# Four-layer cross-attention stack: second half of layer 0 and first FFN fed by runs and block transposes

## The chip, the cores and the metric

The kernel runs on one core of one Trainium2 chip, as one launch. The metric is device time in microseconds (us), the median of several runs. TensorE (PE) does matrix products and 128x128 transposes through the identity, VectorE (DVE), ScalarE (ACT) and GpSimd (POOL) do the rest, and SyncE (SP) issues most DMA transfers, in order.

## The reference, cut to what matters

Eight batches of 128 tokens by 512 features, f32, pass through four layers. Each layer adds a cross attention over a context of the same shape and then an FFN, each fed by a layernorm of the running x.

```python
for layer in range(4):
    x = x + xattn[layer](layernorm(x), ctx)
    x = x + ffn[layer](layernorm(x))

# layer 0's attention: h = layernorm(x)
r = h * rsqrt(mean(h * h) + 1e-5) * ln_weight
q, k, v = r @ w_q.T, ctx @ w_k.T, ctx @ w_v.T        # 32 heads of 128
s = q @ k.T + position_bias                          # per head
p = where(mask, softmax(where(mask, s, -inf)), 0)
out = h + (p @ v).reshape(B, S, 4096) @ w_out.T

# layer 0's FFN: y = layernorm(x)
out = y @ W_base.T + b_base + sum over 8 experts of
      sparsemax(y @ W_router.T)[e] * (y @ lora_A[e]) @ lora_B[e]
```

Layer 1 is a channel attention with small projections and an int8 linear FFN, layer 2 a grouped-query attention with rotary positions (32 heads over 8) and an FFN whose NF4 weights (512 by 1376) are quantised and dequantised in the kernel, layer 3 an attention with normed queries and keys and a gated FFN of low-rank experts.

## The kernel before

The residual lies in on-chip memory as eight tiles `x[b]` of 128 tokens by 512. Products contract over partitions, so every input of a projection is needed with features on the partitions: `ctxT` holds the context of all batches that way ([128, 4 chunks, 8 x 128 tokens]), and the tiles `xT`, made for half the batches at a time, the normed x.

The main loop runs over units. A unit is one head of layer 0's attention (`Unit0`) or layer 2's (`Unit2`) for one half of four batches; the list goes by kind, half, group of four heads, head, so units 0 to 31 are layer 0 with batches 0 to 3 and units 32 to 63 layer 0 with batches 4 to 7. The loop is pipelined: at unit u it projects keys and queries of unit u+3, scores unit u+2, sends that unit's probabilities to DRAM as 32x32 blocks and reads those of u+1 back transposed (`far`, then `pt`), and multiplies unit u's with the values. The first three units take no such detour: their probabilities are transposed by PE (L226) right behind the softmax (L404 to L408). After each fourth head come four projections of values and four output projections.

All that isn't such a unit runs as side work. A table maps slot numbers to functions (`put(i, f)`), and `slot()`, called after each projection and around the values and output projections, runs what stands at the present number and then some NF4 items at a pace (`NF4_PACE`) that differs between stages and between a full and an empty table. `l0_half(1)` fills the table at u = 3 with the preparation of the second half of layer 0; `short_stages(0)` fills it after unit 31 with the first FFN (`F0`), the whole of layer 1 (`L1`, `F1`) and the inputs of layer 2 (`L2Inputs`) for batches 0 to 3, `short_stages(1)` after unit 63 for the other half. `drain()` runs what is left, at u = 29, 61 and 93. The framework orders instructions within each engine anew and places semaphores, so an engine's order is not the program's order word for word, but each engine runs its own list strictly in order.

What the change touches, with the line numbers of the kernel before:

- `transposed` (L187 to L192) makes four PE transposes into one bank, L191.
- `load_ctx` and `l0_ctx` (L354): one load of a batch's context, four PE transposes, an ACT copy into `ctxT` (L355).
- `l0_query` (L366): load of x, `layernorm` (L173: statistics and scaling on DVE, the inverse root on POOL at L160), the rms norm `l0_rms` (L361 a square on ACT, L362 and L364 on DVE), and on POOL x += h (L371).
- `l0_turn` (L374): four PE transposes of the normed rows, and L375 on DVE, which multiplies them by `ln_weight` into `xT0[1]`.
- `norm_sent` and `norm_arrives` (from L258): layernorm, block transpose on DVE (L262), to DRAM, and back in four transfers to a block tile `xB`, features on partitions. It serves later stages already.
- `norm_pieces` (L1193): layernorm in one slot, four PE transposes and an ACT copy (L1200) in the next.
- `l0_half` (L1214), `short_stages` (L1227), and the two first tiles `xT0`, with three warm-up matmuls on the second (L1297 to L1302).

Of the kernel before, what the change touches and what calls it, by code (L numbers as in the profile page):

```python
# [11 lines left out]
F32 = mybir.dt.float32  # L12
# [11 lines left out]
P = 128  # L24
B = 8
D = 512
DC = D // P
NG = 8
HALF = 4
# [33 lines left out]
def kernel(ctx: ExitStack, tc: tile.TileContext, a, out):  # L63
    nc = tc.nc
    V, S, G, T = nc.vector, nc.scalar, nc.gpsimd, nc.tensor

    def pool(name, bufs, **kw):
        return ctx.enter_context(tc.tile_pool(name=name, bufs=bufs, **kw))
# [10 lines left out]
    dram = pool("scratch", 1, space=DRAM)  # L79
# [32 lines left out]
    def load(dst, src):  # L112
        nc.sync.dma_start(dst, src)
# [19 lines left out]
    def along(v, n):  # L133

        return v.unsqueeze(2).to_broadcast([v.shape[0], v.shape[1], n])
# [5 lines left out]
    def batches(hf):  # L141
        return range(hf * HALF, (hf + 1) * HALF)

    def cols(b):
        return slice((b % HALF) * P, (b % HALF + 1) * P)

    def toks(b):
        return slice(b * P, (b + 1) * P)
# [9 lines left out]
    def inv_sqrt(v, shape):  # L158

        return G.tensor_tensor(v, v, mhalf.to_broadcast(shape), ALU.pow)  # L160
# [3 lines left out]
    for b in range(B):  # L164
        t = keep.tile([P, D], F32, name=f"x{b}")
        x.append(t)

    ctxT = keep.tile([P, DC, B * P], F32, name="ctxT")
    lnw = keep.tile([P, DC], F32, name="lnw")
# [5 lines left out]
    def layernorm(st, b):  # L175
        stats = st.small(6, "st")
        V.bn_stats(stats, x[b])
        mv = st.small(2, "mv")
        V.bn_aggr(mv, stats)
        rs = st.small(1, "rs")  # L180
        V.tensor_scalar(rs, mv[:, 1:2], 1e-5, None, ALU.add)  # L181
        inv_sqrt(rs, [P, 1])
        h = st.wide("h")
        V.tensor_scalar(h, x[b], mv[:, 0:1], rs, ALU.subtract, ALU.mult)
        return h

    def transposed(st, src):  # L187

        tp = st.tp()
        for c in range(DC):  # L190
            T.transpose(tp[:, c, :], src[:, c * P:(c + 1) * P], ident)  # L191
        return tp  # L192

    def xt_tile():
        return xtp.tile([P, DC, 512], F32, tag="xT", name="xT")
# [8 lines left out]
    def load_ctx(st, b):  # L204
        c = st.wide("h")
        load(c, a["ctx_4096"][b])
        return c
# [48 lines left out]


    def norm_sent(st, b, quarters=False):  # L258
        h = layernorm(st, b)
        view = "p (a b k) -> p a b k" if quarters else "p (b a k) -> p a b k"  # L260
        tb = st.wide("sq" if st.name == "s" else "pt", (P, 4, DC, 32))
        V.transpose(tb, h.rearrange(view, a=4, k=32))  # L262
        far = dram.tile([4, 32, 4, P], F32, tag="farn", name="far", bufs=4)
        load(far.rearrange("a i b n -> (a i) (b n)"), tb.rearrange("p b c j -> p (b c j)"))
        return far

    def norm_arrives(xB, b, far):
        i = 4 * (b % HALF)
        for q in range(4):
            load(xB[32 * q:32 * q + 32, i:i + 4].rearrange("p a c j -> p a (c j)"), far[:, :, q, :].rearrange("a i n -> i a n"))  # L270

    def xb_tile():
        return xtp.tile([P, 16, DC, 32], F32, tag="xT", name="xB")
# [19 lines left out]
    class Unit:  # L293
# [26 lines left out]
        def send(self):  # L320
            self.arrive = blocks_sent(qkv, self.p, "0", (1, 2))
# [30 lines left out]
            V.tensor_reduce(anyv, m8, AX.X, ALU.max)  # L352

    def l0_ctx(st, b):  # L354
        S.copy(ctxT[:, :, toks(b)], transposed(st, load_ctx(st, b)))  # L355

    def l0_rms(st, h):

        r = st.wide("sq")
        ss = st.small(1, "ss")  # L360
        S.activation(r, h, AF.Square, accum_out=ss)  # L361
        V.tensor_scalar(ss, ss, 1.0 / D, 1e-5, ALU.mult, ALU.add)  # L362
        done = inv_sqrt(ss, [P, 1])
        V.tensor_scalar(r, h, ss, None, ALU.mult)  # L364
        return r, done

    def l0_query(st, b):
        load(x[b], a["x"][b])
        h = layernorm(st, b)
        r, _ = l0_rms(st, h)  # L370
        G.tensor_add(x[b], x[b], h)  # L371
        return r

    def l0_turn(st, b, r):  # L374
        V.tensor_mul(xT0[b // HALF][:, :, cols(b)], transposed(st, r), along(lnw, P))  # L375
# [769 lines left out]
    with ExitStack() as early:  # L1145
# [13 lines left out]
        side = Stream("s", sub_pool("side", 2), ps, {k: ("side", 3) for k in ("mm", "tp", "sc", "pv", "po")})  # L1159
# [5 lines left out]
        xT0, xT2 = [], []  # L1165
# [6 lines left out]
        def put(i, f, *args):  # L1172
            table.setdefault(i, []).append((f, args))
# [20 lines left out]
        def norm_pieces(i, box, b, get, lag=1):  # L1194

            def norm():
                box[b] = layernorm(side, b)

            def turn():
                S.copy(get()[:, :, cols(b)], transposed(side, box[b]))  # L1200

            put(i, norm)
            put(i + lag, turn)

        def norm_blocks(i, b, get, quarters=False):

            box = {}

            def send():
                box[b] = norm_sent(side, b, quarters)  # L1210

            put(i, send)
            put(i + 2, lambda: norm_arrives(get(), b, box[b]))

        def l0_half(hf):
            box = {}

            def query(b):
                box[b] = l0_query(side, b)

            now[0] = 0
            for i, b in enumerate(batches(hf)):
                put(4 * i, l0_ctx, side, b)
                put(4 * i + 1, query, b)
                put(4 * i + 3, lambda b: l0_turn(side, b, box[b]), b)

        def short_stages(hf):  # L1227
            o = {}
            now[0] = 0

            def begin(name, kind, *args):
                o[name] = kind(side, *args)

            def call(i, name, method, *args):
                put(i, lambda: getattr(o[name], method)(*args))

            put(0, begin, "f0", F0, hf)
            box = {}
            for i, b in enumerate(batches(hf)):
                norm_pieces(i, box, b, lambda: o["f0"].xT)  # L1240
                call(i + 3, "f0", "route", b)
                call(i + 9, "f0", "hidden", b)
                call(i + 11, "f0", "output", b)
            call(7, "f0", "gate")
            put(14, lambda: o["f0"].pool.__exit__(None, None, None))
            put(15, begin, "l1", L1, hf)

            for i, b in enumerate(batches(hf)):
                t = 16 + 15 * i
                call(t - 1, "l1", "norm", b)  # L1250
                call(t, "l1", "project", b)
                call(t + 8, "l1", "project_values", b)
                for n, s in enumerate((2, 6, 10, 13)):
                    call(t + s, "l1", "score", b, n)
                    call(t + s + 4, "l1", "arrive", b, n)
                    call(t + s + 9, "l1", "weigh", b, n)
                call(t + 23, "l1", "close", b)
                call(t + (29 if i < 3 else 24), "l1", "output", b)
            t = 16 + 15 * 3 + 24
            put(t, lambda: o["l1"].pools.close())  # L1260
            put(t + 1, begin, "f1", F1, hf)
            def last():
                o["xT"] = (xb_tile, xt_tile)[hf]()
                xT2.append(o["xT"])

            box2 = {}
            put(t + 6, last)
            for i, b in enumerate(batches(hf)):
                call(t + 1 + i, "f1", "norm", b)
                call(t + 3 + i, "f1", "turn", b)  # L1270
                call(t + 4 + i, "f1", "output", b)

                if hf == 0:
                    norm_blocks(t + 6 + i, b, lambda: o["xT"])
                else:
                    norm_pieces(t + 6 + i, box2, b, lambda: o["xT"], 2)
            t = t + 7
            put(t, lambda: o["f1"].pool.__exit__(None, None, None))
            if hf == 0:
                put(t + 1, begin, "l2", L2Inputs)  # L1280
                for b in range(B):
                    call(t + 1 + b, "l2", "gather", b)
                    call(t + 5 + b, "l2", "turn", b)
                put(t + 13, lambda: o["l2"].pool.__exit__(None, None, None))
# [9 lines left out]

        for unit in units[:3]:
            unit.far = False
        xT0 += [xt_tile(), xt_tile()]  # L1297

        V.memset(xT0[1][:, 0, :], 0.0)
        idle = side.mm()  # L1300
        for i in range(3):
            T.matmul(idle, lhsT=xT0[1][:, 0, 0:P], rhs=xT0[1][:, 0, :], start=True, stop=True)  # L1302
        of = {b: (main, side)[b // 2] for b in batches(0)}
        cts = {b: load_ctx(of[b], b) for b in batches(0)}
        for b in batches(0):
# [24 lines left out]
        for u, unit in enumerate(units):  # L1330
            stage[0] = u // (4 * NG)
            turning[0] = 8 * NG - 4 <= u < 8 * NG
            if u == 3:
                l0_half(1)
# [98 lines left out]
    n = len(items)  # L1433
# [117 lines left out]
```

## Time and profile before

| what | us |
|---|---|
| median of 3 runs | 3042.48 (3041.72 to 3043.21) |
| the profiled run's own time | 3044.83 |
| its span | 3042.7 |
| DVE busy | 1901.7 |
| ACT busy | 1347.2 |
| POOL busy | 382.7 |
| granted TensorE clock, mean | 0.999 |

The span is the time from the first to the last recorded instruction of the core; the run's own time also holds what lies around it. Durations in the views below come from that one profiled execution. Lines with an x and a number are groups; a name such as `ctxT<-tp` is output and input. Text in brackets behind an instruction says how long its engine had been idle and what ended the wait.

### The profile page before, as it was taken

Reading aid. Unit: us, or ns where it says so; the run is one execution under the profiler, and the core shown is the slowest. Engines: PE = TensorE matmul, PEld = TensorE weight load, DVE = VectorE, ACT = ScalarE, POOL = GpSimd, SP = SyncE. Lnnn points to the kernel's source line nnn. Section 1 sums busy time; section 2 is a strip of 40 time slices with the busy share of each in tenths; the row PEclk is TensorE's granted clock in tenths of the full one; section 3 lists DMA queues with packets and bytes.
Section 4 is the critical chain, followed back from the end, with each engine's and each line's share of the span. In section 5 each row is a group of like instructions: output and inputs, shape, how many; then the busy total and the mean of one; then the engine's idle time right before and its main releaser. Section 6 shows DMA issues by size and latency. Waiting matters only on the chain.

```text
span 3042.7 us, 35209 instructions
## 1 busy us (share of the span) xinstructions
PE 3011.0 (99%) x10668; PEld 1648.4 (54%) x10672; DVE 1901.7 (63%) x3830; ACT 1347.2 (44%) x3793; POOL 382.7 (13%) x491
## 2 busy tenths in 40 slices
PE   9999999999999999999999999999999999999999
PEld 4544555544444565555555554446666565565554
DVE  5766677667776566887888882215555455555554
ACT  4555565546552533555555660003333434333332
POOL 2000000101110122332111110001111111111110
PEclk9999999999999999999999999999999999999999
DMA  7434444336555633655344443224555655655540
GB/s 217 136 115 125 124 130 125 101 118 166 169 167 165 188 104 103 180 178 178 109 150 132 120 124 95 75 74 144 160 188 176 187 166 169 192 166 178 171 125 14
DMA packets 452796, 433.90 MB, mean 143 GB/s; under 512 B 47968, under 2 KB 343648, under 8 KB 452096
## 3 DMA queue, kind: packets, MB, share of 16 engines
q1 hardware_dynamic: 418432, 355.08, 38.6%
q10 hardware_dynamic: 23040, 41.95, 4.6%
q0 software_dynamic: 11136, 34.61, 3.8%
q8 instruction: 87, 1.43, 0.2%
q14 instruction: 101, 0.83, 0.1%
HBM read 311.93 MB, written 119.56 MB: 142 GB/s over the span
## 4 chain that ended last, share of the span: by engine, by line
PE 86%; DVE 8%; ACT 2%; issue 1%; DMA 1%; POOL 0%; SPq 0%; DVEq 0%; ACTq 0%; POOLq 0%
PE mm L282 18%; PE mm L219 12%; PE po L219 7%; PE mm L417 7%; PE tp L988 7%; PE mm L1011 7%; PE mm L946 5%; PE pv L1071 4%; PE sc L1048 4%; PE pv L330 3%; PE sc L310 3%; PE mm L955 2%; PE mm L714 1%; ACT s L214 1%; PE mm L724 1%
## 5 line engine op out<-in xcount | busy, mean ns | idle before, releaser
L219 PE MATMUL mm<-w,o 128*128 128x512 f32 x1024 | 464.3, 597 | 2.0 <-ACT o L332 1.6
L780 ACT ACTIVATE ind<-nw,bounds 128x512 f32<-128x512 f32 (+2 forms) x495 | 345.1, 712 | 239.1 <-DVE dq L791 162.7
L282 PE MATMUL mm<-xT,w 128*128 128x512 f32 x768 | 346.8, 594 | 3.5 <-DVE rot L704 2.2
L791 DVE SCALAR_TENSOR_TENSOR dq<-ind,dq 128x512 f32<-128x512 f32 (+2 forms) x462 | 327.4, 709 | 27.1 <-ACT ind L780 9.1
L219 PEld LDWEIGHTS mm<-w,o 128*128 128x128 f32 x1024 | 189.2, 191 | 222.4 <-issue 208.0
L214 ACT ACTIVATE s<-s,nm 128x128 f32<-128x128 f32 x512 | 198.2, 388 | 99.0 <-DVE nm L301 94.5
L282 PEld LDWEIGHTS mm<-xT,w 128*128 128x128 f32 x768 | 142.5, 190 | 170.2 <-issue 162.3
L1011 PE MATMUL mm<-w,xT 128*128 128x512 f32 x512 | 233.9, 592 | 0.0
L219 PE MATMUL po<-w,o 128*128 128x512 f32 x512 | 233.2, 594 | 0.0
L282 PE MATMUL mm<-ctxT,w 128*128 128x512 f32 x512 | 230.6, 593 | 1.3 <-ACT ctxT L1306 0.7
L417 PE MATMUL mm<-w,ctxT 128*128 128x512 f32 x512 | 230.5, 593 | 0.0
L214 ACT ACTIVATE p<-sc,nm,rq 128x256 f32<-128x256 f32 x256 | 141.2, 563 | 115.9 <-DVE nm L1053 111.9
L310 PEld LDWEIGHTS sc<-k,q 128*128 128x128 f32 x1024 | 131.5, 191 | 53.0 <-issue 45.1
L219 PEld LDWEIGHTS po<-w,o 128*128 128x128 f32 x512 | 96.3, 190 | 110.6 <-issue 103.1
L417 PEld LDWEIGHTS mm<-w,ctxT 128*128 128x128 f32 x512 | 95.2, 190 | 112.0 <-issue 110.3
L160 POOL TENSOR_TENSOR rs<-rs,mhalf 128x1 f32<-128x1 f32 x64 | 37.8, 593 | 934.1 <-DVE rs L181 923.6
L946 PE MATMUL mm<-xB,w 128*128 128x512 f32 (+1 forms) x352 | 152.3, 592 | 0.8 <-DVE x L220 0.8
L220 DVE TENSOR_TENSOR x<-x,mm 128x512 f32<-128x512 f32 x128 | 86.6, 677 | 104.7 <-PE mm L219 104.5
L1052 DVE TENSOR_REDUCE nm<-sc 128x2 f32<-128x512 f32 x128 | 85.3, 674 | 101.7 <-PE sc L1048 101.4
L282 PEld LDWEIGHTS mm<-ctxT,w 128*128 128x128 f32 x512 | 93.4, 190 | 101.2 <-issue 97.9
L1011 PEld LDWEIGHTS mm<-w,xT 128*128 128x128 f32 x512 | 97.0, 190 | 89.5 <-issue 85.4
L332 ACT COPY o<-pv 128x512 f32<-128x512 f32 x128 | 74.2, 580 | 158.5 <-PE pv L330 158.4
(261 smaller groups left out, 4883.8 us busy)
## 6 DMA issues: line engine op xcount, KB each, us to landing
w<-in_l_wq SPq DMA_DIRECT2D x128, 256.0 KB
w<-in_l_wo SPq DMA_DIRECT2D x128, 256.0 KB
far<-tb SPq DMA_DIRECT2D x125, 256.0 KB
pt<-far SPq DMA_DIRECT2D x500, 64.0 KB
far<-tb SPq DMA_DIRECT2D x60, 512.0 KB
pt<-far SPq DMA_DIRECT2D x240, 128.0 KB
far<-tb SPq DMA_DIRECT2D x63, 384.0 KB
pt<-far SPq DMA_DIRECT2D x252, 96.0 KB
```

The lines of the kernel that those rows point to most:

```text
L214: S.activation(dst(h), src(h), AF.Exp, bias=negm[:, h:h + 1], scale=by, accum_out=su[:, h:h + 1])
L219: T.matmul(mm, lhsT=o(h), rhs=wo[h], start=h == 0, stop=h == 3)
L282: T.matmul(mm, lhsT=w[:, c, :], rhs=chunk(xT, c), start=c == 0, stop=c == DC - 1)
L310: T.matmul(sc[:, i, :], lhsT=self.q[:, i * P:(i + 1) * P], rhs=k[:, i * P:(i + 1) * P], start=True, stop=True)
L417: T.matmul(mm, lhsT=ctxT[:, c, toks(self.hf * HALF + i)], rhs=grp.wv[c], start=c == 0, stop=c == DC - 1)
L780: S.activation(ind, w, AF.Relu, bias=bounds[:n, i:i + 1], scale=(down + up)[i][1])
L791: V.scalar_tensor_tensor(dst, ind, step, dst, ALU.min, ALU.subtract if i == len(down) else ALU.add)
L946: T.matmul(mm[:n, :], lhsT=w[c][:, j * P:j * P + n], rhs=chunk(xT, c), start=c == 0, stop=c == DC - 1)
L988: T.matmul(it.kv[:, s, :], lhsT=lhsT, rhs=it.wkv[c // 2][:, c % 2, :], start=c == 0, stop=c == DC - 1)
L1011: T.matmul(mq, lhsT=self.xT[it.hf][:, c, cols(it.b)], rhs=it.wq[c], start=c == 0, stop=c == DC - 1)
L1048: T.matmul(sc[:, i, :], lhsT=it.qT[2 * j + i], rhs=it.kT, start=True, stop=True)
L1071: T.matmul(pv, lhsT=it.v[:, j, :], rhs=it.pts[j], start=j == 0, stop=j == 1)
```

## The change

Three things are done differently for parts of the work.

The context of batches 4 to 7 is read straight from the input in runs of 128 bytes, by four transfers a batch (`runs_back`), so that each 32x32 block lies where one block transpose on DVE (`runs_turned`) leaves it transposed in `ctxT`.

The rms-normed rows of these batches are block-transposed on DVE (`blocks_out`, split out of `norm_sent`), sent to DRAM, read back in four transfers into a block tile (`norm_arrives`), and multiplied there by `ln_weight` on POOL (`l0_weigh`). `xT0[1]` becomes such a block tile. The steps of one batch are now spread over ten slots and batches start six slots apart; before, it was four slots each.

In the first FFN of batches 0 to 3 (`hf == 0`) the layernormed rows go to DRAM whole (`runs_sent`), come back two slots later in runs of 128 bytes, and are block-transposed two slots after that (`norm_runs`). All later slots of `short_stages(0)` move by three; `short_stages(1)` stays as it was. In the loop over `L1` a variable is renamed because `s` is now the shift.

```diff
--- before.py
+++ after.py
@@ -256,8 +256,9 @@
 
 
     def norm_sent(st, b, quarters=False):
-        h = layernorm(st, b)
-        view = "p (a b k) -> p a b k" if quarters else "p (b a k) -> p a b k"
+        return blocks_out(st, layernorm(st, b), "p (a b k) -> p a b k" if quarters else "p (b a k) -> p a b k")
+    def blocks_out(st, h, view):
         tb = st.wide("sq" if st.name == "s" else "pt", (P, 4, DC, 32))
         V.transpose(tb, h.rearrange(view, a=4, k=32))
         far = dram.tile([4, 32, 4, P], F32, tag="farn", name="far", bufs=4)
@@ -268,6 +269,25 @@
         i = 4 * (b % HALF)
         for q in range(4):
             load(xB[32 * q:32 * q + 32, i:i + 4].rearrange("p a c j -> p a (c j)"), far[:, :, q, :].rearrange("a i n -> i a n"))
+    def runs_sent(src, queue):
+        far = dram.tile([P, D], F32, tag="farr", name="far", bufs=4)
+        queue.dma_start(far, src)
+        return far
+    def runs_back(st, far, queue):
+        t = st.wide("h", (P, DC, 4, 32))
+        src = far.rearrange("(k j) (c a e) -> a j c k e", j=32, c=DC, e=32)
+        for q in range(4):
+            queue.dma_start(t[32 * q:32 * q + 32], src[q])
+        return t
+    def runs_turned(dst, t):
+        V.transpose(dst.rearrange("p c (k j) -> p c k j", j=32), t)
 
     def xb_tile():
         return xtp.tile([P, 16, DC, 32], F32, tag="xT", name="xB")
@@ -352,7 +372,10 @@
             V.tensor_reduce(anyv, m8, AX.X, ALU.max)
 
     def l0_ctx(st, b):
-        S.copy(ctxT[:, :, toks(b)], transposed(st, load_ctx(st, b)))
+        return runs_back(st, a["ctx_4096"][b], nc.sync)
+    def l0_ctx_turn(b, t):
+        runs_turned(ctxT[:, :, toks(b)], t)
 
     def l0_rms(st, h):
 
@@ -370,6 +393,14 @@
         r, _ = l0_rms(st, h)
         G.tensor_add(x[b], x[b], h)
         return r
+    def l0_send(st, b, r):
+        return blocks_out(st, r, "p (b a k) -> p a b k")
+    def l0_weigh(b):
+        i = 4 * (b % HALF)
+        t = xT0[1][:, i:i + 4]
+        G.tensor_mul(t, t, lnw.unsqueeze(1).unsqueeze(3).to_broadcast([P, 4, DC, 32]))
 
     def l0_turn(st, b, r):
         V.tensor_mul(xT0[b // HALF][:, :, cols(b)], transposed(st, r), along(lnw, P))
@@ -1202,6 +1233,20 @@
             put(i, norm)
             put(i + lag, turn)
 
+        def norm_runs(i, b, get):
+            box = {}
+            def send():
+                box[b] = runs_sent(layernorm(side, b), nc.sync)
+            def back():
+                box[b] = runs_back(side, box[b], nc.sync)
+            put(i, send)
+            put(i + 2, back)
+            put(i + 4, lambda: runs_turned(get()[:, :, cols(b)], box[b]))
         def norm_blocks(i, b, get, quarters=False):
 
             box = {}
@@ -1219,10 +1264,19 @@
                 box[b] = l0_query(side, b)
 
             now[0] = 0
+            def ctx_load(b):
+                box[b, 0] = l0_ctx(side, b)
+            def send(b):
+                box[b, 1] = l0_send(side, b, box[b])
             for i, b in enumerate(batches(hf)):
-                put(4 * i, l0_ctx, side, b)
-                put(4 * i + 1, query, b)
-                put(4 * i + 3, lambda b: l0_turn(side, b, box[b]), b)
+                put(6 * i, ctx_load, b)
+                put(6 * i + 2, query, b)
+                put(6 * i + 4, lambda b: l0_ctx_turn(b, box[b, 0]), b)
+                put(6 * i + 4, send, b)
+                put(6 * i + 7, lambda b: norm_arrives(xT0[1], b, box[b, 1]), b)
+                put(6 * i + 9, l0_weigh, b)
 
         def short_stages(hf):
             o = {}
@@ -1235,28 +1289,32 @@
                 put(i, lambda: getattr(o[name], method)(*args))
 
             put(0, begin, "f0", F0, hf)
-            box = {}
+            box, s = {}, 3 * (1 - hf)
             for i, b in enumerate(batches(hf)):
-                norm_pieces(i, box, b, lambda: o["f0"].xT)
-                call(i + 3, "f0", "route", b)
-                call(i + 9, "f0", "hidden", b)
-                call(i + 11, "f0", "output", b)
-            call(7, "f0", "gate")
-            put(14, lambda: o["f0"].pool.__exit__(None, None, None))
-            put(15, begin, "l1", L1, hf)
+                if hf == 0:
+                    norm_runs(i, b, lambda: o["f0"].xT)
+                else:
+                    norm_pieces(i, box, b, lambda: o["f0"].xT)
+                call(i + s + 3, "f0", "route", b)
+                call(i + s + 9, "f0", "hidden", b)
+                call(i + s + 11, "f0", "output", b)
+            call(s + 7, "f0", "gate")
+            put(s + 14, lambda: o["f0"].pool.__exit__(None, None, None))
+            put(s + 15, begin, "l1", L1, hf)
 
             for i, b in enumerate(batches(hf)):
-                t = 16 + 15 * i
+                t = s + 16 + 15 * i
                 call(t - 1, "l1", "norm", b)
                 call(t, "l1", "project", b)
                 call(t + 8, "l1", "project_values", b)
-                for n, s in enumerate((2, 6, 10, 13)):
-                    call(t + s, "l1", "score", b, n)
-                    call(t + s + 4, "l1", "arrive", b, n)
-                    call(t + s + 9, "l1", "weigh", b, n)
+                for n, d in enumerate((2, 6, 10, 13)):
+                    call(t + d, "l1", "score", b, n)
+                    call(t + d + 4, "l1", "arrive", b, n)
+                    call(t + d + 9, "l1", "weigh", b, n)
                 call(t + 23, "l1", "close", b)
                 call(t + (29 if i < 3 else 24), "l1", "output", b)
-            t = 16 + 15 * 3 + 24
+            t = s + 16 + 15 * 3 + 24
             put(t, lambda: o["l1"].pools.close())
             put(t + 1, begin, "f1", F1, hf)
             def last():
@@ -1294,12 +1352,13 @@
 
         for unit in units[:3]:
             unit.far = False
-        xT0 += [xt_tile(), xt_tile()]
-        V.memset(xT0[1][:, 0, :], 0.0)
+        xT0 += [xt_tile(), xb_tile()]
+        dummy = xT0[1][:, 0:4].rearrange("p a c j -> p (a c j)")
+        V.memset(dummy, 0.0)
         idle = side.mm()
         for i in range(3):
-            T.matmul(idle, lhsT=xT0[1][:, 0, 0:P], rhs=xT0[1][:, 0, :], start=True, stop=True)
+            T.matmul(idle, lhsT=dummy[:, 0:P], rhs=dummy, start=True, stop=True)
         of = {b: (main, side)[b // 2] for b in batches(0)}
         cts = {b: load_ctx(of[b], b) for b in batches(0)}
         for b in batches(0):
```

## The prediction

> **What bounds the kernel now.** I read the head of the page first, for the busy time of each engine and the chain that ended last.
>
> ```profile
> span 3042.7 us, 35209 instructions
> PE 3011.0 (99%) x10668; PEld 1648.4 (54%) x10672; DVE 1901.7 (63%) x3830; ACT 1347.2 (44%) x3793; POOL 382.7 (13%) x491
> ...
> PE 86%; DVE 8%; ACT 2%; issue 1%; DMA 1%; POOL 0%; SPq 0%; DVEq 0%; ACTq 0%; POOLq 0%
> ```
>
> TensorE (PE) is busy for 3011.0 of 3042.7 us, so about 31.7 us of the whole span are not matrix work, and the next engine, VectorE (DVE), has a third of its time free. The averages say nothing about the stages that the change touches, so next came the table of busy time by stretches (length, then PE, PEld, DVE, ACT and POOL with counts, granted clock, DMA share, GB/s).
>
> ```profile
> 0.00:60.00 60.00, 55.40 (x175) 27.95 (x176) 30.50 (x80) 21.14 (x51) 16.30 (x42) 1.00 0.82 255
> 60.00:140.00 80.00, 80.00 (x271) 42.04 (x270) 59.82 (x111) 51.45 (x120) 5.43 (x6) 1.00 0.39 119
> ...
> 550.00:640.00 90.00, 90.00 (x297) 46.83 (x296) 48.50 (x116) 29.42 (x75) 5.29 (x7) 1.00 0.33 99
> ```
>
> The second half of layer 0 is prepared in the second row and the first FFN's norms run in the third: PE is busy for 80.00 of 80.00 and 90.00 of 90.00 us, at full clock. What leaves PE there leaves the span, and whatever makes PE wait is added to it. VectorE has 20 and 41 us free, the DMA engines more than half. Third, the chain of waits from 60 us on (start, length, what):
>
> ```profile
> 77.54 3.44 PE mm L282 x8
> 80.98 0.44 PE tp L191 x4
> 81.42 3.44 PE mm L282 x8
> ```
>
> The transposes of a context tile stand between two projections without a gap, 0.44 us the four. Eight such groups lie between 80.98 and 141.4; four more in the first FFN (at 558.44, 564.10, 568.90, 575.49) are each followed 0.44 us later by the next matmul. Last, the timeline of VectorE and PE where the first score is worked on (start, length, instruction):
>
> ```profile
> 40.41 0.15 DVE L181 TENSOR_SCALAR rs<-mv 128x1 f32<-128x1 f32 x1
> 45.85 0.69 DVE L404 TENSOR_TENSOR s<-sc,bias 128x512 f32<-128x512 f32 x1 [5.28 <-PE sc L310]
> ...
> 50.10 0.69 DVE L408 TENSOR_TENSOR s<-s,su 128x512 f32<-128x512 f32 x1
> ```
> ```profile
> 50.94 0.63 PE L226 MATMUL tp<-ident,s 128*128 128x128 f32 x4
> ```
>
> VectorE waits 5.28 us for the first score and its softmax runs straight through; PE takes the result at 50.94, 0.15 us after L408 ends (50.10 + 0.69). There is no slack in this one softmax: the later units read their probabilities back through DRAM one unit later, the first has its matmuls right behind it.
>
> **What goes.** PE loses 12 groups of four transposes, 8 in the second half of layer 0 and 4 in the first FFN: 12 x 0.44 = 5.28 us, all on the path. ACT loses 8 copies (L355 584 ns, L1200 586 ns) and DVE 4 multiplications (L375, 684 ns); neither is on the path, worth 0.
>
> **What comes on VectorE and GpSimd.** Twelve block transposes, 128x512: the same instruction takes 704 ns at L262. 12 x 0.70 - 4 x 0.68 = 5.7 us more on DVE, beside PE work, worth 0 while they keep from delaying a softmax. Four multiplications by lnw on POOL, priced by L371 (1274 ns): 5.1 us on an engine that is busy 5.43 of 80 us. The first such L371 at 82.31 ran beside a DVE L408 that took 1.80 instead of 0.69 us, so each may stretch one DVE operation by 1.1 us; the softmaxes there have a unit of PE work (about 9 us from one score to the next in the chain) as cover, so 0, up to 1.1 if that cover is gone. [...]
>
> **What comes on the DMA queues.** SP issues some 53 transfers more. A context batch becomes four transfers of 512 runs of 128 bytes; in the packet records a 128-byte packet takes 13 ns against 84 for 2 KB, so a batch costs 2048 x 13 / 16 = 1.7 us of all engines where 128 x 84 / 16 = 0.7 did, in a stretch at 0.39. The nearest transfer of many small runs, the gather of amr (4 x 512 runs of 44 bytes, issued from 991.91), had landed at 996.09, 4.2 us later. Data sent to DRAM and read back costs 2.06 us from the sending to the first issue of the reading (far at 74.83, pt at 76.89). Queries and contexts of the second half are first used more than 300 us later (three units ahead of unit 32), so their latency is worth 0. [...]
>
> **The start: a new wait.** In the changed program's order two things move ahead of the first score. SP's loads of x4 and x5 (at 28.05 before) now stand behind the second load of values, which waits for PE and goes out at 34.65; x4 goes out at about 35.0. And before L404 VectorE has the first context's block transpose, both batches' norms and one more block transpose. x4 lands 3.6 us after its issue (x7: issued 35.84, its statistics released at 39.47), at 38.6; bounds 37.1 (the 2.06 above) and 38.9 (x4's own 3.85). From the first statistics to the scaled row took 6.36 us (31.90 to 38.26), about 6.0 without one of the two rs in POOL's way; then the block transpose 0.70, the second h 0.53, its square 0.7 on ACT, which waits beside a POOL addition of 1.27, ss 0.15 + 0.55, and the scaling 0.48: 3.6. So the first score is taken at 38.6 + 9.6 = 48.2 instead of 45.85, 2.35 us late, and PE at L226 with it: +2.35 (0.85 to 3.1). Queued behind it on VectorE are the next softmax, with 3 us to spare, and one NF4 weight. Another block transpose falls between row maximum and reciprocal of this softmax; the 1.72 us wait for ACT there hides its 0.70.
>
> **The first FFN.** Layernormed rows go to DRAM, come back two slots later and are turned two slots after that; everything behind moves by three slots. PE waits are possible where `route` meets the fourth turn, which stands behind a softmax and an NF4 step on VectorE (I work out 0.3 to 0.4), and where a key weight's load is issued only just ahead of use, behind a send that waits for its data (0 to 0.5). Together +0.5 (0 to 1.5). The last slot becomes 108 of about 116 before the drain, so no work falls into the drain.
>
> **The reshuffle.** Side work of units 32 to 61 shifts, and about four of 462 NF4 items (L791) come later and are caught up. PE's idle spots behind it, 2.0 us in 940 to 1000 and 17.5 in 1060 to 1840, may change: 0, with 3 either way.
>
> **Sum.** Against the profiled run's own 3044.83 (span 3042.7): -5.28 + 2.35 + 0.5 = -2.4, 3042.4. The median of the runs is 3042.48, 2.35 lower, so 3040.0 in that measure.
>
> **Rivals.** 0.2% is 6.1 us, about what this measurement tells from no change; its bounds are 3036.4 and 3048.6.
>
> A (the sum, 0.55): 3040.0; with the terms' bounds 3036 to 3044.
>
> B, the gain comes whole and the new order helps (0.22): x4 lands in time or PE's order hides the late softmax, 3042.48 - 5.28 = 3037.2; with 3 us off the idle spots, 3034. For it: PE has 17.5 us of idle in the stretch behind. Against: the 0.15 us of slack at 50.94.
>
> C, a wait on read-backs takes the place of the transposes (0.13): VectorE is in order, and a block transpose that waits for its four transfers holds the softmaxes behind it. Place: the eight turns at 80 to 145 and 555 to 600 us. Two slots are about 7 us (two groups of 3.44) against 4.2 to land. If landing takes 9, each turn is 2 us late, 8 x 2 = 16: 3040.0 + 16 = 3056; slower than before from 7.3 us on (8 x 0.3 = 2.4), beyond 0.2% from 8.1. Against: 0.33 to 0.39 DMA share; for: SP issues in order, and sends that wait for data stand ahead of the read-backs.
>
> D, the transposes were hidden anyway (0.10): only the new waits remain, 3042.48 + 2.35 + 0.5 = 3045.3. Against: PE 80.00 of 80.00 and no gap in the chain.
>
> **How the numbers follow.** Forecast 3040.0. Faster by over 0.2%: the better part of B and a little of A, 0.18. Slower: C from 8.1 us on and an unseen reshuffle, 0.12. Within: 0.70. The range 3035 to 3047 holds A, most of B, D and the mild end of C, 0.8.
>
> **What would show it.** Right: 48 fewer transposes at L191's line and PE busy about 3006; the first softmax's L404 near 48 us and PE idle some 2.3 us before the first L226; no PE idle between 60 and 550. Wrong: PE idle beside the block transposes of ctxT or f0's xT, a read-back longer than 7 us, or idle in 940 to 1840 far from 19.5 us.

## The result, and the profile after

| | before | after |
|---|---|---|
| median of 13 runs each, us | 3042.65 (3041.66 to 3045.11) | 3051.68 (3045.54 to 3054.83) |
| profiled run's own time / its span, us | 3044.83 / 3042.7 | 3048.9 / 3047.0 |

The ratio is 1.0023, with a 95% interval of 1.0016 to 1.0030: the change costs some 7 us (the two medians lie 9.0 apart), and the runs spread over 9 us where they spread over 3.5. The forecast of 3040.0 was wrong in size and sign. The profiled run is one of the quicker ones of the changed kernel, so its own 4.1 us do not hold the whole loss.

The head of the page of the kernel after:

```profile
span 3047.0 us, 35185 instructions
...
PE 3008.7 (99%) x10624; PEld 1645.3 (54%) x10624; DVE 1905.6 (63%) x3838; ACT 1343.1 (44%) x3785; POOL 386.2 (13%) x495
...
PE 80%; DVE 11%; ACT 3%; issue 2%; DMA 2%; POOL 1%; SPq 0%; DVEq 0%; ACTq 0%; POOLq 0%
```

PE's busy time fell by 2.3 us and the span grew by 4.3: PE stands still for 6.6 us more. Where, the table of stretches of the kernel after shows (length, then PE, PEld, DVE, ACT and POOL with counts, granted clock, DMA share, GB/s):

```profile
0.00:60.00 60.00, 54.70 (x170) 27.66 (x171) 31.79 (x79) 20.69 (x51) 18.04 (x43) 1.00 0.79 222
60.00:140.00 80.00, 79.62 (x258) 41.01 (x257) 62.00 (x118) 49.90 (x117) 8.70 (x9) 1.00 0.59 171
...
550.00:640.00 90.00, 89.24 (x282) 45.56 (x281) 46.76 (x113) 29.51 (x75) 3.46 (x5) 1.00 0.45 126
...
1000.00:1060.00 60.00, 57.77 (x179) 28.83 (x178) 30.72 (x69) 29.05 (x73) 7.81 (x8) 0.97 0.69 209
1060.00:1840.00 780.00, 757.75 (x3329) 436.33 (x3328) 618.92 (x1073) 403.68 (x1322) 168.87 (x185) 1.00 0.45 137
```

and the same two late stretches of the kernel before:

```profile
1000.00:1060.00 60.00, 60.00 (x187) 30.10 (x186) 36.04 (x70) 34.80 (x82) 3.02 (x3) 1.00 0.71 205
1060.00:1840.00 780.00, 762.53 (x3338) 438.08 (x3340) 617.91 (x1078) 400.96 (x1318) 171.74 (x187) 1.00 0.45 137
```

In the stages where transposes were replaced PE lost little: 0.7, 0.4 and 0.8 us more idle. The largest piece lies more than 400 us behind the last replaced transpose, in 1060 to 1840 us, where idle grew from 17.5 to 22.3. In 1000 to 1060 us, where it was 0, it is 2.2, and there the seventh column has a clock of 0.97 where it was 1.00.

The start, on VectorE and on PE of the kernel after (start, length, instruction, in brackets the wait before it):

```profile
37.54 0.69 DVE L177 BATCH_NORM_STATS2 st<-x 128x6 f32<-128x512 f32 x1 [4.87 <-DMA x<-in_x]
...
46.25 0.49 DVE L387 TENSOR_SCALAR sq<-h,ss 128x512 f32<-128x512 f32 x1 [0.94 <-POOL ss L160]
46.65 0.68 DVE L435 TENSOR_TENSOR s<-sc,bias 128x512 f32<-128x512 f32 x1
...
50.91 0.69 DVE L439 TENSOR_TENSOR s<-s,su 128x512 f32<-128x512 f32 x1
```
```profile
51.74 0.63 PE L226 MATMUL tp<-ident,s 128*128 128x128 f32 x4 [1.81 <-DVE s L439]
...
78.18 3.60 PE L302 MATMUL mm<-ctxT,w 128*128 128x512 f32 x8
81.62 3.60 PE L302 MATMUL mm<-xT,w 128*128 128x512 f32 x8
...
583.90 1.17 PE L491 MATMUL mm<-wra,xT 128*128 128x136 f32 x8 [0.27 <-DVE xT L290]
585.55 3.70 PE L302 MATMUL mm<-xB,w 128*128 128x512 f32 x8 [0.49 <-DMA w<-in_l_wq]
...
1009.45 0.44 PE L727 MATMUL tp<-ident,csrow 128*128 128x128 f32 x2 [2.23 <-DMA csrow<-in_rope,row]
1009.72 5.29 PE L302 MATMUL mm<-xB,w 128*128 128x512 f32 x8
...
1834.59 1.13 PE L350 MATMUL pv<-pt,v 128*128 128x128 f32 x8 [2.11 <-DMA pt<-far]
```

The norms of the first two new batches (L177 to L387) stand ahead of the first score (L435), and PE waits 1.81 us for that softmax. At 78 to 85 us the two projections now follow each other with no transposes between them. The first FFN has two small waits. The long ones are below them: layer 2's gathered rotary rows (csrow) and, last, a read-back of probabilities (pt). The csrow wait was there before, shorter (`issue` means that the profile shows nothing that ended it; POOL had begun the gather 3.65 us before, about the least that one took to land in that profile, 3.6):

```profile
997.25 0.41 PE L696 MATMUL tp<-ident,csrow 128*128 128x128 f32 x2 [1.43 <-issue]
```

**Clock dips.** The granted clock of ten microseconds around that csrow wait, in the kernel after:

```profile
1010.00:1020.00 10.00, 10.00 (x34) 5.34 (x33) 4.73 (x8) 3.84 (x10) 2.84 (x3) 0.83 0.91 270
```

The clock records behind this column show 0.5 for 3.41 us at a time. Within such a dip the 128x512 matmuls of one projection start 0.86 us apart instead of 0.43 (the line at 1009.72 above: 5.29 us where 3.60 is usual). So a dip costs half its length, 1.7 us, of work that is bound by PE, and in a table of busy time it looks like busy PE. Each run's mean clock is recorded to three digits, so (1 - clock) x 3045 us estimates what dips cost it. The estimate is coarse: in the profiles 0.999 is one dip or two (1.7 or 3.4 us) and 0.998 is three; four would round to it as well. Over the runs of both kernels with a clock on record (23 after, 129 before): before, 3044.4 us on average of which 1.4 are dips; after, 3051.4 of which 6.0 are dips. Of the loss of 7 us, some 4.5 are clock by this estimate (3.5 to 5.8 if each clock is read as its fewest or its most dips), and some 2.5 are waits less work saved. The second number agrees with the profile: 5.28 forecast as saved, 7.3 more idle up to 1840 us, 2.0 net.

### The profile page after: what moved, and what is told of

The parts are those of the page before. It is cut to its first block, busy times and chain, and to the rows that moved or that the text cites. A ratio compares the mean times of both kernels' runs of the same rounds, so it can differ in the third digit from the quotient of the medians.

```text
span 3047.0 us, 35185 instructions
## 1 busy us (share of the span) xinstructions
PE 3008.7 (99%) x10624; PEld 1645.3 (54%) x10624; DVE 1905.6 (63%) x3838; ACT 1343.1 (44%) x3785; POOL 386.2 (13%) x495
## 4 chain that ended last, share of the span: by engine, by line
PE 80%; DVE 11%; ACT 3%; issue 2%; DMA 2%; POOL 1%; SPq 0%; DVEq 0%; ACTq 0%; POOLq 0%
PE mm L302 16%; PE mm L219 10%; PE po L219 7%; PE tp L1019 7%; PE mm L1042 7%; PE mm L448 7%; PE mm L977 5%; PE pv L1102 4%; PE sc L1079 4%; PE mm L986 2%; PE pv L350 2%; PE sc L330 2%; DVE dq L822 2%; ACT s L214 2%; DVE tb L241 1%
## 5 line engine op out<-in xcount | busy, mean ns | idle before, releaser
L302 PE MATMUL mm<-xT,w 128*128 128x512 f32 x512 | 230.8, 594 | 4.7 <-DVE rot L735 3.3
L302 PE MATMUL mm<-xB,w 128*128 128x512 f32 x512 | 233.9, 599 | 0.5 <-DMA w<-in_l_wq 0.5
L302 PEld LDWEIGHTS mm<-xT,w 128*128 128x128 f32 x512 | 95.2, 190 | 116.3 <-issue 109.3
L302 PEld LDWEIGHTS mm<-xB,w 128*128 128x128 f32 x512 | 95.1, 191 | 110.9 <-issue 107.9
```

The costliest lines, as they stand in the source:

```text
L302: T.matmul(mm, lhsT=w[:, c, :], rhs=chunk(xT, c), start=c == 0, stop=c == DC - 1)
```

## The experiments

All were timed against the kernel before on the same chip. "Dips" is the estimate just given, "rest" the mean less dips; since the clock has three digits, either can be off by up to some 1 us. The expectations name rival theories T1, T2 and so on; each says what it means there, and T2 stands for one thing in a0, b and c and for another in h and behind it. The kernel before had a dip share of 1.0 to 1.7 and a rest of 2.8 to 3.0 above 3040 in every group of runs.

| kernel | median (runs) | ratio, 95% interval | dips | rest above 3040 |
|---|---|---|---|---|
| the change again (a0) | 3050.90 (10) | 1.0022, 1.0013 to 1.0031 | 6.7 | 5.2 |
| only layer 0 (b) | 3042.96 (11) | 1.0004, 0.9995 to 1.0012 | 1.7 | 3.3 |
| only first FFN, with shift (c) | 3048.83 (12) | 1.0016, 1.0008 to 1.0025 | 2.8 | 7.1 |
| only the shift (d) | 3054.06 (7) | 1.0030, 1.0019 to 1.0041 | 4.8 | 8.1 |
| late slots unshifted (e) | 3050.63 (11) | 1.0018, 1.0009 to 1.0027 | 4.7 | 6.5 |
| NF4 pace (f) | 3045.90 (11) | 1.0002, 0.9993 to 1.0011 | 2.8 | 2.8 |
| csrow turned later (g) | 3043.29 (11) | 0.9999, 0.9990 to 1.0008 | 2.5 | 0.9 |
| norms behind the score (h) | 3048.21 (11) | 1.0012, 1.0003 to 1.0021 | 5.8 | 2.3 |
| g and h (i) | 3041.07 (11) | 0.9991, 0.9982 to 1.0000 | 3.3 | -1.4 |
| f, g and h (k) | 3040.46 (11) | 0.9987, 0.9978 to 0.9996 | 3.9 | -2.7 |
| before, csrow turned earlier (j) | 3046.43 (11) | 1.0008, 0.9999 to 1.0018 | 2.8 | 4.2 |
| before, csrow turned later (l) | 3043.45 (11) | 0.9992, 0.9983 to 1.0001 | 0.0 | 2.8 |
| b and g (m) | 3046.24 (11) | 1.0009, 1.0000 to 1.0018 | 3.1 | 3.5 |
| b, g and h (n) | 3042.31 (11) | 0.9993, 0.9984 to 1.0002 | 2.5 | -0.2 |
| d and g (q) | 3043.55 (11) | 0.9997, 0.9988 to 1.0006 | 1.7 | 2.1 |
| before, csrow turned two earlier (p) | 3047.90 (11) | 1.0012, 1.0003 to 1.0021 | 2.2 | 5.5 |

### The change again, and its parts alone

a0 is the changed kernel, unedited.

> The changed kernel again, for a second profile of it and its spread. Theory T1 (the loss sits in waits on nearly late transfers and results between 940 and 1850 us, at other places from run to run, each long one followed by a dip of the granted clock): median 3048 to 3054, PE idle in 1060 to 1840 us above the 17.5 us of before by 4 us or more, and at least two dips of the clock where before's profile has one. Rival T2 (the start stall and the read-backs of layer 0's second half cost it): PE idle of 5 us or more between 0 and 640 us beyond before's 4.6.

Five dips in one execution, all in these windows of a0's profile (columns as above):

```profile
50.00:60.00 10.00, 7.67 (x23) 3.63 (x22) 8.58 (x18) 5.36 (x20) 1.58 (x1) 0.83 0.23 60
1010.00:1020.00 10.00, 7.56 (x21) 3.41 (x20) 4.16 (x8) 4.21 (x14) 5.02 (x6) 0.83 0.79 233
1210.00:1220.00 10.00, 8.99 (x38) 4.33 (x39) 8.84 (x18) 7.13 (x32) 3.70 (x6) 0.83 0.35 122
1240.00:1250.00 10.00, 8.97 (x22) 3.81 (x22) 7.27 (x15) 4.90 (x23) 2.94 (x5) 0.83 0.62 178
1840.00:1850.00 10.00, 7.46 (x20) 3.48 (x19) 3.09 (x8) 0.59 (x1) 0.71 (x2) 0.83 0.16 47
```

and these are PE's waits at four of the five places in the same run's timeline:

```profile
54.00 0.63 PE L226 MATMUL tp<-ident,s 128*128 128x128 f32 x4 [2.33 <-DVE s L439]
...
1013.91 0.44 PE L727 MATMUL tp<-ident,csrow 128*128 128x128 f32 x2 [2.44 <-DMA csrow<-in_rope,row]
...
1211.01 1.13 PE L350 MATMUL pv<-pt,v 128*128 128x128 f32 x8 [1.37 <-ACT s L214]
...
1842.49 1.13 PE L350 MATMUL pv<-pt,v 128*128 128x128 f32 x8 [1.86 <-DMA pt<-far]
```

The dips begin at 55.2, 1014.4, 1212.3, 1243.1 and 1843.8 us. Four of them begin 0.5 to 1.3 us after the start of one of these lines; the one at 1243.1 follows two waits of 0.60 and 0.43 us in a stretch of small matmuls. So the same kernel is quick or slow in good part by the number of its dips: this run took 3056.8 us with five, the profile shown above 3048.9 with two, and three dips are 5.1 of these 7.9 us. PE's idle time in 1060 to 1840 is 20.0 us, 2.5 above before's; but the read-back wait of 1.86 us lies just behind 1840 here, and up to 1860 it is 23.4 against 18.2, the 5 us that T1 expected. T2's 5 us before 640 did not come (3.2).

Kernel b keeps only the part in layer 0:

```diff
-            box, s = {}, 3 * (1 - hf)
+            box, s = {}, 0
-                if hf == 0:
-                    norm_runs(i, b, lambda: o["f0"].xT)
-                else:
-                    norm_pieces(i, box, b, lambda: o["f0"].xT)
+                norm_pieces(i, box, b, lambda: o["f0"].xT)
```

> Only the part in layer 0's second half (context in runs, rms rows through DRAM); the first FFN as before, no shift by three slots. T1: the gain of 8 groups less the start stall, 3042.6 - 3.5 + 2.2 = 3041.3 (3040 to 3043). T2: slower than before, 3046 or more, since the culprit is in it.

3042.96 against 3043.95 of the kernel before on that chip, 1.0 lower, but the interval holds no change, and also T2's 3046 (1.0007): seven runs lie at 3041.4 to 3043.2 and four at 3047.6 to 3052.0. The median fits T1 and speaks against T2, no more. Kernel c is the other part: `l0_half`, `l0_ctx` and `xT0[1]` as before, `norm_runs` and the shift kept.

> Only the first FFN's norms through DRAM with all later slots three later; layer 0's second half as before. T1: most of the loss is here, 3047 to 3054. T2: 3042.6 - 1.8 + 0.8 = 3041.6.

It loses 4.9 us of the 7.0 that a0 loses against the same runs of the kernel before. Kernel d is the kernel before with the one line of the shift:

```diff
-            box = {}
+            box, s = {}, 3 * (1 - hf)
```

and `s` added to the slots as in the change; no transpose leaves PE.

> The kernel before with nothing but the later slots of the first short stages moved by three; all transposes stay on PE. T1 with the shift as the cause: slower than before by 4 us or more, 3047 to 3052. T3 (the read-backs of the first FFN themselves, more DMAs in SP's order, are the cause, not the shift): 3042.6 as before, within 1.5.

3054.06, above T1's range: a move of side work by three slots, with not one instruction added, costs as much as the whole change or more. T3 fell here. PE's timeline of d has the csrow wait again, in this execution without a dip behind it:

```profile
1011.84 0.44 PE L727 MATMUL tp<-ident,csrow 128*128 128x128 f32 x2 [2.58 <-DMA csrow<-in_rope,row]
```

### What in the shift

Kernel e moves only the first FFN and layer 1's first batch:

```diff
-                t = s + 16 + 15 * i
+                t = (s if i == 0 else 0) + 16 + 15 * i
-            t = s + 16 + 15 * 3 + 24
+            t = 16 + 15 * 3 + 24
```

> The changed kernel, but only the first FFN and layer 1's first batch move by three slots; everything from layer 1's second batch on stays at its old slot. T1 (the shift of the late slots is the cause): PE idle in 1060 to 1860 us back from 22.3 to about 18, the wait for csrow back from 2.2 to about 1.4 us, 0 to 1 dips of the clock before the end, median 4 us or more below the changed kernel's, about 1.5 to 3 us below the kernel before. T3 (the first FFN's read-backs are the cause): like the changed kernel, 3049 to 3052.

A miss as a test: the time is what T3 expected, which d had ruled out. In its profile the csrow wait is 1.16 us, as expected, and idle in 1460 to 1860 fell to 9.3 from 11.9; but in 1060 to 1460 it rose to 12.8 from 11.2, so that 1060 to 1860 has 22.1 and not the expected 18. And the crowded batches of layer 1 brought waits of their own,

```profile
717.96 0.65 PE L630 MATMUL pv<-pt,vt 128*32 128x128 f32 x16 [1.56 <-DVE s L612]
743.89 1.13 PE L350 MATMUL pv<-pt,v 128*128 128x128 f32 x8 [0.86 <-DMA pt<-far]
```

and dips at 1209 and 1240 us; the time didn't move. Kernel f gives back the NF4 items that the shift puts off (on VectorE's list, where all stages together have 495, 352 of them are begun by the end of layer 0, 356 before; the table is filled for three slots longer, at 1.1 items a slot and not 2.4):

```diff
-        NF4_PACE = ((2.4, 2.4), (1.1, 2.4), (0.0, 1.4), (1.4, 1.4))
+        NF4_PACE = ((2.4, 2.4), (1.137, 2.4), (0.0, 1.4), (1.4, 1.4))
```

> The changed kernel with the pace of NF4 items in layer 0's second half raised from 1.1 to 1.137 a slot, which makes up the four items (352 against 356 done by the end of that stage). T1a (the four late items cause the waits in 1460 to 1860 us): PE idle there back from 11.5 to about 9, the wait for csrow still 2.2 to 2.6 us; median 2 to 4 us below the changed kernel. T1b (the place of the late slots is the cause, not the items): no change, 3050 to 3052.

5 us below the changed kernel's medians. The stretch behind layer 0's end, in the kernel before, after, and f:

```profile
1460.00:1840.00 380.00, 371.54 (x1469) 213.61 (x1468) 312.96 (x512) 213.56 (x604) 64.08 (x51) 1.00 0.42 126
```
```profile
1460.00:1840.00 380.00, 368.93 (x1460) 212.65 (x1459) 314.49 (x509) 216.18 (x608) 61.66 (x49) 1.00 0.42 127
```
```profile
1460.00:1840.00 380.00, 371.52 (x1486) 214.78 (x1484) 314.22 (x513) 216.21 (x612) 63.09 (x49) 1.00 0.42 127
```

PE idle is 8.5, 11.1 and again 8.5 us: where four items fall makes 2.6 us of waits in layer 2, 500 us after they were put off. That they come late isn't the reason, as all 18 profiles show together:

| items begun by the end of layer 0 | profiles | PE idle in 1460 to 1860, us |
|---|---|---|
| 356 | before, b, e, f, j, p | 8.5 to 9.3 |
| 355 | k, l, m, n | 9.7 to 11.3 |
| 352 | after, a0, c, d, h | 11.0 to 11.9 |
| 351 | g, i, q | 7.8 to 9.1 |

The idle time goes by the number of items, but not up with their lateness: one item fewer than the changed kernel has is as good as four more. The items also moved the csrow wait, which is 0.38 us in f's profile, so T1b isn't excluded by f. Kernel g leaves the pace and moves the transposes of csrow by one slot:

```diff
-                    call(t + 5 + b, "l2", "turn", b)
-                put(t + 13, lambda: o["l2"].pool.__exit__(None, None, None))
+                    call(t + 6 + b, "l2", "turn", b)
+                put(t + 14, lambda: o["l2"].pool.__exit__(None, None, None))
```

> The changed kernel with the transposes of the gathered csrow rows one slot later. T1b: PE's wait for csrow (2.2 us) goes and with it the dip of the clock near 1005 us (1.7 us): median 2 to 4 us below the changed kernel. T1a: only that wait goes, 0 to 2 us.

More than expected: no csrow wait at all in its profile, no dip at that place, and a median some 8 us below the changed kernel's, level with the kernel before. But the edit also puts off one NF4 item (351 for 352), and idle in 1460 to 1860 is 7.8 us for 11.9, so that g doesn't tell T1a from T1b. The same edit on the shift alone (q):

> The kernel before with nothing but the shift by three slots (3054 alone), and the csrow transposes one slot later. If the shift costs through the csrow wait and the dips behind it: 3043 to 3046, mean clock 0.9993 or more. If it costs through places that this wait has no part in: 3048 or more.

3054.06 became 3043.55. PE's busy time in d and then in q, at that place:

```profile
1000.00:1060.00 60.00, 57.38 (x181) 28.77 (x180) 33.08 (x73) 29.05 (x73) 7.83 (x8) 1.00 0.68 206
```
```profile
1000.00:1060.00 60.00, 59.88 (x191) 30.32 (x190) 32.07 (x72) 28.61 (x73) 8.15 (x8) 1.00 0.70 209
```

2.5 us of idle in one profile don't make 10 us. What else went with it: dips (4.8 to 1.7 us by the estimate), idle in 1460 to 1840 from 10.5 to 8.3 (351 items for 352, as in g), and what the csrow wait was in runs that weren't profiled, which isn't known. On the kernel before the edit (l) does little to the median:

> The kernel before with the csrow transposes one slot later. If the later turn mends only what the shift brought: 0 to 1.5 us below the kernel before (its own wait of 1.4 us). If it is a gain of its own for any version: 4 us or more below, as for the changed kernel (7 us).

0.7 us lower, within its expected 0 to 1.5, and no dip in any of 11 runs. So the later turn mends what the shift brought, the csrow wait and the items' places together; no run changes one of them alone with the shift kept.

### The start, and the dips

Kernel h issues layer 0's second norms behind the latest score (the load of x leaves `l0_query` for that):

```diff
             def query(b):
-                box[b] = l0_query(side, b)
+                load(x[b], a["x"][b])
+                with tc.issue_after(mark[0].ins):
+                    box[b] = l0_query(side, b)
```

> The changed kernel with layer 0's second norms issued behind the latest score, so that the first softmax isn't held. T2 (the start stall costs its own length, and a clock dip where it is above 2 us): PE's wait of 1.8 to 2.3 us at the first L226 goes and PE idle before 60 us falls from 5.3 to about 4; median 2 to 3 us below the changed kernel. T1 says the same for this term, and that the rest of the loss, 5 us or more against the kernel before, stays.

2.7 to 3.5 us below the changed kernel, and still slower than before, as both theories said, by 4.0 us where T1 had 5 or more. The clean pair is m and n, layer 0's part without the shift and with the later turn; they differ in this edit alone:

> Only the part in layer 0's second half, with the csrow transposes one slot later; the start wait of 1.8 to 2.3 us is in it. From the kernel before with the later turn (3043.5, its mean clock 1.0000): -3.5 for 8 groups of transposes, +1.9 start wait, and where T4 holds a dip behind the start wait in some runs: 3041.5 to 3043 with a mean clock of 0.9994 to 0.9999. If dips have nothing to do with that wait: clock 1.0000.

> The same with layer 0's second norms behind the latest score. T4 and T2's price: no PE wait at the first L226, mean clock 1.0000, 3039.5 to 3041, 2 us or more below the version with the start wait. If the start wait had cover after all: the same within 1 us.

PE's timeline of m and then of n:

```profile
52.33 0.63 PE L226 MATMUL tp<-ident,s 128*128 128x128 f32 x4 [2.12 <-DVE s L439]
```
```profile
50.47 0.63 PE L226 MATMUL tp<-ident,s 128*128 128x128 f32 x4
```

The wait of 2.12 us is gone, and 3.9 us of the median with it (3046.24, 3042.31; the means differ by 4.2, of which 3.7 is rest and the remainder dips). The 0.72 us that PE waited between 60 and 140 us in m's profile are gone in n's too; where the last us lies isn't shown. Both levels are above what was expected, m by 3 us and n by 1.3, and n's clock is not 1.0000: its profile has a dip at 1233.1 us.

Kernels j and p turn csrow earlier in the kernel before (t + 4 + b and t + 3 + b in the line above), to lengthen its wait:

> The kernel before with the csrow transposes one slot earlier, which lengthens PE's wait for them from 1.4 us by one slot to some 4 to 5 us and changes nothing else of weight. T4 (a PE wait above about 2 us is followed by a dip of the granted clock to half for 3.4 us, which costs 1.7 us more): a dip within 2 us of that wait in the profile, mean clock lower by 0.0006 or more, median 4 to 6 us above the kernel before. Rival (dips come at random times and not from waits): no dip there, median 3 to 3.5 us above.

> The kernel before with the csrow transposes two slots earlier, so that PE must wait 4 us or more for the gathered rows (1.4 before). T4: a wait longer than the 3.4 us of a dip brings a dip behind it in every run, mean clock 0.9990 or less; median 3044.1 + 2.6 + 1.7 or more = 3048.4 or more. If waits and dips aren't tied: clock 0.9995 as before, 3046.7.

The waits didn't grow as meant: 2.33 us in j, and in p

```profile
994.41 0.41 PE L696 MATMUL tp<-ident,csrow 128*128 128x128 f32 x2 [2.31 <-issue]
```

with a dip behind it in p's profiled run and none in j's. Both profiled runs are the quickest of their 11, so the waits may have been longer in others. The medians are above the kernel before's by 2.3 us (j, whose interval still reaches 1) and 4.2 us (p), with 356 items begun as before and only the turns moved; the dips' share rose by 1.2 us in each, which fits neither "always" nor "not tied".

Over the 18 profiles there are 25 dips apart from those at the very end; each begins during a PE wait or within 1.9 us behind the end of one, places that make up about 3% of the spans, so dips at random times are ruled out. Of 21 PE waits of 1.8 us or more, 11 are followed by a dip. Within one run they begin whole multiples of 3.413 us apart (a0: 1014.4 - 55.2 = 959.2 = 281 x 3.413), and in the 13 profiles that have both, the dip at the very end lies on the same grid; so each profile's own grid can be read off.

What counts shows when each span is cut into the windows of its grid and PE's idle time is added up in each (the first 15 and the last 12 us aside). All 11 windows with 2.04 us of idle or more (2.04 to 2.44) are followed by a dip. Of the 158 with 1.0 to 2.0 us 14 are, 13 of them between 1199 and 1243 us; of the windows with less, none, but for the second half of two double dips. So in these profiles a wait is punished whenever some 2 us of it fall into one window, and a wait as long can escape when the grid cuts it in two: 2.56 us in h, up to 1007.0, with at most 1.90 in one window. Why less is enough around 1199 to 1243 us, and once at 1835 (m, 1.64 us), is not shown. None of the waits here was as long as a window (the longest is the 2.58 us in d), and 2.04 us of idle in one was enough.

### A version that beats both

i has g and h on the changed kernel, k has f as well.

> The changed kernel with both repairs, layer 0's second norms issued behind the latest score and the csrow transposes one slot later. If start wait and csrow wait are separate terms (T1 with T2's start stall): the 3043.3 of the later turn less 1.8 to 2.3 and less the clock dips behind the start wait, 3039.5 to 3042, faster than the kernel before by 2 to 4 us. If the waits only move: 3043 to 3046.

> The same with the NF4 pace of 1.137 as well (355 items done by the end of layer 0 in place of 351). If the items' places in layer 2 matter by their number: PE idle in 1460 to 1860 us near 9, against 7.5 with 351: 1 to 2 us slower than the version with both repairs. If all waits are settled by the first two: the same within 1 us.

That the two waits are separate terms fits: i is within its 3039.5 to 3042, though its interval reaches 1.0000. k is the quickest of the sixteen and clear of 1, 3040.46 against 3044.12 of the kernel before in the same group of runs, ratio 0.9987 (0.9978 to 0.9996); that its pace adds something over i isn't shown. Its page:

```profile
span 3039.9 us, 35181 instructions
...
PE 3007.1 (99%) x10624; PEld 1645.1 (54%) x10624; DVE 1903.0 (63%) x3838; ACT 1343.0 (44%) x3785; POOL 391.1 (13%) x495
```

Its rest is 5.7 us below that of the kernel before in the same group, and 5.5 below that of l, which has the later turn alone; the forecast gain was 5.28. Its dips are 2.3 us above.

## Why the prediction was wrong

**Right: the gain.** 48 transposes are gone at L191 (136 to 104 of h, 24 to 8 of the normed rows), PE goes from projection to projection, and where the waits are mended (k, i) the rest falls by 5.7 and 4.3 us, by an estimate good to some 1 us. PE's busy time was to be near 3006 and is 3008.7; one dip more than in the profile before holds 1.7 of that. That PE was the bound was read rightly; D falls.

**Right: the start wait, its size in part by luck.** Forecast 2.35 us (0.85 to 3.1), through x4's late load; measured 1.81, 2.12 and 2.33 in profiles (after, m, a0), and 3.9 us of median in the pair m and n. x4 landed at 37.5 and not 38.6, and the path to the score took 9.1 and not 9.6 us, so that the score was taken at 46.65 and not 48.2, 0.80 us late against the profile before. The other 1.0 of the 1.81 came from PE, which reached its wait that much earlier than in the profile before; the forecast had no such term.

**Right: the first FFN.** Forecast 0.5 us at `route` and at a weight's load; 0.27 and 0.49 at just these two places. Rival C had the sign and the wrong place: none of the block transposes held PE longer than this 0.27.

**Wrong: the term for the reshuffle, "0, with 3 either way".** This is the step that failed. The four late NF4 items were seen and counted, and then said to be "caught up". They are, in layer 2, and there the five profiles with 352 items begun have 11.0 to 11.9 us of idle where the six with 356 have 8.5 to 9.3; that 351 are as good as 356 shows that it is their places that count. The csrow wait was also in the numbers, as part of the 2.0 us of idle before, without asking what comes of it when its slots fall elsewhere: from 1.4 it became 2.2 to 2.6 us (after, a0, c, d, h), with a dip behind it in three of these five profiles. The gather was no slower: POOL begins it at 993.60 us before and 1006.06 after, and the transposes start 3.65 and 3.39 us later; but of this time PE had other work for 2.2 us before and for 1.2 us after. Idle in 940 to 1840 grew by 5.0 us in the profiled run, and kernel d priced the whole shift alone at 9 us (ratio 1.0030, 1.0019 to 1.0041), three times the 3 that the term allowed either way. How these 9 us divide between the items' places, the csrow wait and the dips is an estimate at best. Where a step moves hundreds of instructions, zero was no value to take for it, since these stages had 19.5 us of idle that hung on where things fall.

**Missing: the clock.** The sum had no term for it. The kernel before shows 0.999 in its profile, one dip at 1237 us, and it was passed over. A wait's price was taken as its length; with a dip it is 1.7 us more, and by the estimate some 4.5 of the 7 us came so.

**Not settled.** Why less than 2 us of idle in a window is enough for a dip at some places; how long the csrow wait is in runs that were not profiled, which p's median suggests to be longer than the one seen; and why the read-backs of probabilities in 1200 to 1330 us wait 0.2 to 2.4 us from one execution or variant to the next.

## What to carry to other kernels

A table of side work that is placed slot by slot has waits tuned into it: a shift by a few slots is a change of its own, and is best tried alone, with no other edit, before its cost is put at nothing. Where PE is the bound, take each wait's length plus, from some 2 us on, a chance of 1.7 us for the clock (here a dip came behind 11 of 21 waits of 1.8 us or more), and look at every run's clock, not only at the profiled one, when runs begin to spread. A gain on PE is kept only if the work that replaces it isn't ordered ahead of what PE waits for next; naming the instruction behind which it may be issued was enough here (m and n, 2.12 us of wait and 3.9 us of the median).

## What the runs showed that was not expected

The granted clock halves for 3.413 us at a time behind PE waits of 0.4 to 2.5 us, on a grid of the same length, though PE is 99% busy over the run; a window of that grid with 2.04 us of idle or more was followed by a dip every time. Two dips in a row were seen as one of 6.8 us (i and k, at 1202.4 and 1199.9). Some lie behind waits of only 0.4 to 0.6 us, all in the stretch of 1230 to 1245 us, where layer 1's scores are matmuls with 32 rows of weights (0.70 us for four); with one dip in it this is the only place where the profile of the kernel before shows one.
